# Softmax denominators of a convolution-attention block taken group by group in 64x64 tiles, two scalings and one run of silus moved

## The chip, the cores and the metric

The kernel runs on one core of one Trainium2 chip. The metric is the device time of one execution in microseconds (us), as the median of repeated runs; lower is better. Three runs of the kernel before took 2205.79, 2205.89 and 2208.82 us.

The core has a matrix engine (PE, with its weight loads shown apart as PEld), a vector engine (DVE), a scalar engine (ACT), a third engine for simple vector work (POOL) and a queue engine that mostly issues transfers (SP). Each takes its instructions strictly in order; semaphores tie the engines together. Matrix products write to PSUM, eight banks per partition; everything else lives in SBUF or in DRAM.

## The reference

All data is float32: eight images of 512 channels, 32x32 pixels. After a group norm comes one block with a residual:

```python
t = cbs(x, cv1_w, cv1_bn, 0)              # 1x1 convolution, batch norm, silu
ys = [t[:, :C], t[:, C:]]                 # C = 256
for i in range(N):                        # N = 2
    yi = ys[-1]
    z = cbs(yi, m_cv1_w[i], m_cv1_bn[i], 1)          # 3x3 convolution
    z = bot_attention(z, m_qkv_w[i], m_rw[i], m_rh[i])
    z = jax.nn.silu(bn_eval(conv2d(z, m_cv2_w[i], 0), m_cv2_bn[i]))
    ys.append(yi + z)
out = x + cbs(jnp.concatenate(ys, axis=1), cv2_w, cv2_bn, 0)

# in bot_attention: 4 heads of 64 channels, hw = 1024 positions
logits = jnp.einsum('bhdi,bhdj->bhij', q, k + r) * HD ** (-0.5)
a = jax.nn.softmax(logits, axis=-1)
out = jnp.einsum('bhij,bhdj->bhdi', a, v)
```

What matters here is the softmax: its denominator is the sum of exp(logits) over the 1024 keys j, for each of 4 heads and 1024 queries i.

## The kernel before

Images go in four pairs (loop variable `p`, images `ia` and `ib`), and each pair goes through the two rounds n = 0 and n = 1. So there are 16 attentions, one for each image and round, in the order n=0 `ia`, n=0 `ib`, n=1 `ia`, n=1 `ib` of each pair; counted from 0 in time they are called attention 0 to 15 below. Between them stand the 3x3 convolutions (L675), the q, k, v projections (`project_strassen`, a seven-product scheme, or `project_direct`), the 1x1 convolution behind each attention (`m2`, L1336), the first convolution of the next images (`strassen_cv1`, whose handle is called `nxt`) and the last convolution.

One attention (`attention_fast`, from L1058) has four **groups**: two channel blocks `c` (each with two heads) times two halves of the queries (512 each). A group has eight key blocks j of 128, taken as four **pairs**. For each key block, four matrix products in 64x64 tiles write the logits of both heads (`l_ps`, 128 keys x 1024, L1082), ACT takes the exponential into `pt` (L1086), DVE adds `pt` onto `acc` (L1100, L1103), and four products in 64x64 tiles accumulate with v (`av_ps`, L1119). Every float32 product stands as two matmul instructions in the trace, so that a key block has 8 for the logits and 8 for v, and a pair 16 and 16. The loop is skewed: the logits of pair i are issued before the product with v of pair i-1. At the end of a group ACT copies half of `av_ps` into `z`, and DVE adds the other half (L1126, L1127).

`acc` then holds sums over the eight key blocks, one for each of the 128 partitions and both heads; the sum over the partitions is still missing. `sums` (L1129) makes it with a matrix product by ones: four products per group that use all 128 rows and 32 columns each, over 256 elements, so 8 matmul instructions per group. `batch` says which groups go together: mostly (0, 1) and (2, 3); where `apart` or `at_once` is set (2,) and (3,) go alone. A group that is not the last of its batch and not in an `apart` or `at_once` attention has its last addition held back (`held_back`, L1101) until the group's `av_ps` has been evicted (L1225). ACT copies the row sums (`s_row`, L1143), SP stores them in DRAM (L1144), loads them in another layout (`total`, L1171), DVE takes the reciprocal (L1179), SP stores and loads it spread over partitions (`rs`, L1181, L1186), and DVE multiplies `z` (`scale`, L1195). `last_sums` (L1147) is another way, used in attention 0 alone (`at_once`): 64x64 tiles, two halves of the keys apart.

Where the sums stand: those of (0, 1), and of (2,) where it is alone, between the logits and the product with v of the next group (L1218, L1219); those of the last batch are called by the code after the attention (`end.sums()`), behind the first product of what follows. The groups (0, 1) are scaled inside the last group (L1214). `end.spread()` and `end.scale()` do the last batch, before `m2`.

`apart` is set for n=0 `ib` (attentions 1, 5, 9, 13); eleven attentions are plain; attention 0 is `at_once`.

The tile framework orders the instructions of each engine with a planner that simulates the engines with estimated costs, and inserts the semaphore waits and buffer releases. `tc.issue_after(ins)` only says that an instruction stands behind another on the same engine. Pools have fixed buffers by tag: three two-bank PSUM buffers `big` (logits, sums, most other products), one two-bank `av`; in SBUF `acc` 2, `h` 2 (row sums, and temporaries of the convolution's tiles), `rs` 4, `pt` 6.

Two further places belong to the change. `finish` (L1897) runs six silus on ACT for the next image's first convolution; in the n=1 attentions it is called from `middle` behind the silus of `m2` and ahead of the exponential's table load. `first_tiles` (L2188) makes the first tiles for the 3x3 convolution near the start; POOL clears two edge columns (L591, L592) that DVE needs (L619).

Of the kernel before, what the change touches and what calls it, by code (L numbers as in the profile page):

```python
# [45 lines left out]
F32 = mybir.dt.float32  # L46
# [16 lines left out]
def kernel(  # L63
# [449 lines left out]
    def stages(act, small, ps_big, ps_av, n_pt):  # L513
# [425 lines left out]
        def project_strassen(n, z, w, t, early=None, middle=None, table=False, silus=()):  # L939
# [80 lines left out]
            if table:  # L1020
                with tc.issue_after(copied.ins):
                    table_of(AF.Exp)
            ps_c, ps_w = big(), big()
# [34 lines left out]
        def attention_fast(qkv, ao, at, behind, at_once=False, apart=False):  # L1058
# [70 lines left out]
            def sums(gs):  # L1129

                NQ4 = HALF // 2
                ps = ps_big.tile([P, len(gs), NQ4], F32, tag="big", name="s_ps")
                for n, g in enumerate(gs):
                    acc = accs.pop(g)
                    for at_q in range(4):
                        hd, part = divmod(at_q, 2)
                        nc.tensor.matmul(  # L1137
                            ps[at_q * 32 : (at_q + 1) * 32, n, :], ones[:, 0:32], acc[:, hd, ts(part, NQ4)],
                            start=True, stop=True, tile_position=(0, at_q * 32),
                        )  # L1140
                s_dram = tc.dram_tile([len(gs), 4, NQ4], F32, name=f"s_dram{at + gs[0]}")
                row = act.tile([P, len(gs), NQ4], F32, tag="h", name="s_row", bufs=2)
                nc.scalar.copy(row, ps)  # L1143
                nc.sync.dma_start(s_dram.rearrange("g a i -> a g i"), row[0:P:32])  # L1144
                return s_dram

            def last_sums(g):  # L1147

                ps = ps_big.tile([P, 2, HALF], F32, tag="big", name="s_ps")
                acc = accs.pop(g)  # L1150
                for kh in range(2):
                    r = slice(kh * HD, (kh + 1) * HD)
                    for hd in range(2):
                        nc.tensor.matmul(
                            ps[hd * HD : (hd + 1) * HD, kh, :], ones[r], acc[r, hd, :],
                            start=True, stop=True,
                        )
# [8 lines left out]
            def last_total(g, s_dram):  # L1166
                cs = small.tile([P, 2, QP], F32, tag="cs", name="cs", bufs=2)
                nc.sync.dma_start(cs, s_dram.rearrange("k h (i r) -> (h i) k r", r=QP))
                nc.vector.tensor_tensor(sums_all[:, at + g, :], cs[:, 0], cs[:, 1], ALU.add)
# [6 lines left out]
            def spread(gs, s_dram):  # L1176

                rc = small.tile([P, len(gs), QP], F32, tag="rc", name="rc", bufs=2)
                inverted[0] = nc.vector.reciprocal(rc, total(gs, s_dram))  # L1179
# [23 lines left out]
            s_drams, rss, evicted = {}, {}, [None]  # L1203
            for i in range(len(pairs) + 1):
                if i < len(pairs):
                    added = logits(pairs[i])
                    g, at_q = divmod(i, NQ)
                    with tc.issue_after(added.ins):
                        if at_q == NQ - 2 and g - 1 in batch:
                            gs = batch[g - 1]  # L1210
                            rss[gs] = spread(gs, s_drams[gs])
# [20 lines left out]
            with tc.issue_after(added.ins):  # L1232
                behind.get(len(groups), lambda: None)()

            g = len(groups) - 1
            if not at_once:
                gs = batch[g]
                if apart:
                    with tc.issue_after(evicted[0].ins):
                        scale_all(batch[g - 1])  # L1240
                return SimpleNamespace(
                    evicted=evicted[0], added=added,
                    sums=lambda: s_drams.update({gs: sums(gs)}),
                    spread=lambda: rss.update({gs: spread(gs, s_drams[gs])}),
                    scale=lambda: scale_all(gs),
                )
            ps, rows, s_dram = last_sums(g)
            with tc.issue_after(added.ins):
                behind.get(len(groups) + 1, lambda: None)()
# [5 lines left out]
            return SimpleNamespace(scaled=scale(g, rs), check=lambda: last_total(g, s_dram))  # L1255
# [559 lines left out]
        def strassen_cv1(w, xts, y0s, y1, t_tile):  # L1815
# [81 lines left out]
            def finish():  # L1897
                with tc.issue_after(silu_in[-1].ins), tc.issue_after(m2_silu[0].ins):
# [289 lines left out]
    def first_tiles(g, i):  # L2188
        return s.tiles_steps(Y1[g], putter(vs, g), [i], ecs[g], ec_at=(("rs", 4), ("t", 4))[g])
# [83 lines left out]
    for p in range(NP):  # L2273
# [166 lines left out]
        if more and not direct:  # L2440
            end.sums()
            nxt.go_on()
            nxt.sums()
# [11 lines left out]
            nxt.finish()  # L2455
# [5 lines left out]
        else:  # L2461
# [30 lines left out]
            else:  # L2492
                qkv = s.project_strassen(
                    0, z[:, :, 1], take_blocks("sq", 0, 1, SQ_NAMES), t, early=end.sums, middle=middle
# [49 lines left out]
        end.sums()  # L2544
# [83 lines left out]

        def middle():
# [3 lines left out]
            if more:  # L2633
                nxt.finish()
                nxt.keep()
# [3 lines left out]
            1, z[:, :, 1], take_blocks("sq", 1, 1, SQ_NAMES), t, early=end.sums, middle=middle  # L2639
# [45 lines left out]
        if not more:  # L2685
# [30 lines left out]
            end.sums()  # L2716
# [79 lines left out]
        end.sums()  # L2796
# [148 lines left out]
```

## Time and profile before

| | before |
|---|---|
| median of three runs | 2205.89 us |
| the profiled execution's own time | 2206.25 us |
| its span in the trace | 2204.8 us |
| PE busy | 2176.4 us (99%) |
| DVE, ACT, POOL busy | 1817.5, 1094.1, 220.9 us |
| TensorE clock granted, mean | 0.999 of full speed |

The span runs from the first to the last instruction that the profiler recorded; the execution takes 1.45 us more. Matmuls are pipelined: one of 512 elements lasts about 590 ns from start to end, but the next starts long before that, so PE's cost is read from the distances between the starts of blocks, and not from the sum of durations. A row of the timeline view gives start and length in us, engine, line, operation, output<-inputs, tile shape (rows*columns) and the operand's shape, a count, and in brackets the idle time ahead of it with its releaser.

### The profile page before, as it was taken

To read this page: it belongs to the slowest core of one execution; us is meant where nothing else is said; L and a number is where in the kernel's file an instruction comes from. 1 tells how busy PE (TensorE), PEld (TensorE's weight loads), DVE (VectorE), ACT (ScalarE), POOL (GpSimd) and SP (SyncE) were. 2 spreads that over 40 slices of the span, in tenths; PEclk is the share of its full clock that TensorE was granted. 3 is DMA by queue.
4 is the path that set the end of the run, shared out by engine and by line. 5 is a ranking of instruction groups with operands and counts; after the bars stand their busy time and mean duration, and the time that the engine had idled before them with its cause. 6 is when DMAs were issued, how large, how long until landed. Compare 5 with 4: busy or idle time off the path is not lost.

```text
span 2204.8 us, 40989 instructions
## 1 busy us (share of the span) xinstructions
PE 2176.4 (99%) x16546; PEld 1117.9 (51%) x16546; DVE 1817.5 (82%) x2996; ACT 1094.1 (50%) x1320; POOL 220.9 (10%) x393
## 2 busy tenths in 40 slices
PE   7999999999999999999999999999999999999998
PEld 3653438343484444734458443564346834383436
DVE  8988879878978688986897868997788877897677
ACT  7454553554225666366314676455622465336543
POOL 4322210000210000000012000000002100000001
PEclk9999999999999999999999999999999999999999
DMA  9954447212583323612159141542126811261224
GB/s 276 323 159 143 163 149 262 84 52 74 153 287 95 118 84 127 208 51 77 57 135 330 33 165 38 184 140 78 59 68 170 301 30 45 92 204 32 76 59 116
DMA packets 135529, 291.93 MB, mean 132 GB/s; under 512 B 33732, under 2 KB 61376, under 8 KB 134308
## 3 DMA queue, kind: packets, MB, share of 16 engines
q1 hardware_dynamic: 102708, 201.01, 27.4%
q0 software_dynamic: 32624, 88.23, 13.6%
q8 instruction: 132, 2.16, 0.4%
q14 instruction: 65, 0.53, 0.1%
HBM read 219.58 MB, written 69.60 MB: 131 GB/s over the span
## 4 chain that ended last, share of the span: by engine, by line
PE 87%; DVE 8%; DMA 2%; issue 1%; ACT 1%; POOL 0%; SPq 0%; DVEq 0%; ACTq 0%; POOLq 0%
PE av_ps L1119 19%; PE l_ps L1082 18%; PE c_ps L675 10%; PE p_ps L958 7%; PE c L1356 5%; PE m_ps L1336 5%; PE c_q L1404 5%; PE x_ps L1828 4%; PE ps L545 3%; PE c L1388 3%; PE p_ps L964 3%; PE c_new L1356 2%; PE s_ps L1137 1%; DMA taps<-in_m_cv_w_dram 1%; DVE acc L1103 1%
## 5 line engine op out<-in xcount | busy, mean ns | idle before, releaser
L1086 ACT ACTIVATE pt<-l_ps 128x1024 f32<-128x1024 f32 x512 | 495.6, 1023 | 328.2 <-PE l_ps L1082 252.4
L1082 PE MATMUL l_ps<-q,kr 64*64 64x512 f32 x4096 | 485.5, 590 | 0.9 <-ACT pt L1086 0.9
L1119 PE MATMUL av_ps<-pt,vT 64*64 64x512 f32 x4096 | 484.7, 590 | 1.2 <-DVE z L1127 1.1
L1103 DVE TENSOR_TENSOR acc<-acc,pt 128x1024 f32<-128x1024 f32 x362 | 442.5, 1222 | 37.2 <-ACT pt L1086 9.8
L1119 PEld LDWEIGHTS av_ps<-pt,vT 64*64 64x64 f32 x4096 | 156.0, 133 | 280.7 <-issue 234.8
L1082 PEld LDWEIGHTS l_ps<-q,kr 64*64 64x64 f32 x4096 | 157.4, 133 | 270.3 <-issue 246.4
L675 PE MATMUL c_ps<-v_in,u 128*64 128x128 f32 x4320 | 238.5, 273 | 0.0
L675 PEld LDWEIGHTS c_ps<-v_in,u 128*64 128x64 f32 x4320 | 235.8, 137 | 4.9 <-issue 4.6
L1127 DVE TENSOR_TENSOR z<-av_ps,z 128x512 f32<-128x512 f32 x64 | 43.9, 687 | 98.6 <-ACT z L1126 98.5
L1336 PE MATMUL m_ps<-z,m_sb 128*128 128x512 f32 x256 | 114.2, 593 | 0.4 <-DVE z L1195 0.4
L958 PE MATMUL p_ps<-t_z,sq 128*128 128x512 f32 x224 | 105.9, 595 | 0.0
L680 ACT COPY c_m<-c_ps 128x512 f32<-128x512 f32 x48 | 28.1, 586 | 151.0 <-PE c_ps L675 132.7
L517 ACT ACTIVATE t<-m_ps,bh,sh 128x512 f32<-128x512 f32 x64 | 46.3, 774 | 95.4 <-PE m_ps L1336 94.2
L1100 DVE TENSOR_TENSOR acc<-pt 128x1024 f32<-128x1024 f32 x64 | 78.0, 1219 | 14.2 <-PE s_ps L1137 8.7
L958 PE MATMUL p_ps<-z,sq 128*128 128x512 f32 x168 | 81.3, 604 | 0.8 <-ACT z L517 0.7
L1336 PEld LDWEIGHTS m_ps<-z,m_sb 128*128 128x128 f32 x256 | 47.7, 190 | 57.4 <-issue 52.3
L1504 POOL DMA_DIRECT2D c_out<-in_x_dram x48 | 43.4, 1041 | 273.6 <-ACT c_out L517 271.9
L1195 DVE TENSOR_TENSOR z<-z,rs 128x512 f32<-128x512 f32 x64 | 42.2, 685 | 30.0 <-DMA rs<-r_dram 29.9
L517 ACT ACTIVATE z<-z,bh,sh 128x512 f32<-128x512 f32 x64 | 48.7, 809 | 25.2 <-DVE z L737 25.1
L958 PEld LDWEIGHTS p_ps<-t_z,sq 128*128 128x128 f32 x224 | 39.5, 191 | 36.6 <-issue 34.4
L517 ACT ACTIVATE c_out<-c,bh,sh 128x512 f32<-128x512 f32 x12 | 14.0, 1280 | 85.7 <-PE c L1388 77.7
L1828 PE MATMUL x_ps<-t_x,sw 128*128 128x512 f32 x128 | 55.9, 592 | 0.0
(409 smaller groups left out, 3326.7 us busy)
## 6 DMA issues: line engine op xcount, KB each, us to landing
u<-u SPq DMA_DIRECT2D x135, 512.0 KB
y_in<-y SPq DMA_DIRECT2D x32, 512.0 KB
rs<-r_dram SPq DMA_DIRECT2D x126, 128.0 KB
sq<-sq SPq DMA_DIRECT2D x42, 384.0 KB
x<-in_x_dram SPq DMA_DIRECT2D x28, 512.0 KB
r_in<-r SPq DMA_DIRECT2D x28, 512.0 KB
c_out<-in_x_dram POOLq DMA_DIRECT2D x56, 256.0 KB, 6.4
out_dram<-c_out POOLq DMA_DIRECT2D x56, 256.0 KB, 5.4
```

The lines of the kernel that those rows point to most:

```text
L517: silued[0] = nc.scalar.activation(dst, src, AF.Silu, scale=sh[:, k : k + 1], bias=bh[:, k : k + 1])
L675: conv_product[0] = nc.tensor.matmul(to[o], us[cp][:, k, row, c, o], rhs, start=(k == 0), stop=(k == NM - 1),)
L958: nc.tensor.matmul(ps[:, o, :], w[:, o, :], rhs, start=not onto, stop=True, skip_group_check=onto)
L1082: nc.tensor.matmul(ps[kh * HD : (kh + 1) * HD, hd, :], kr[r, c, o : o + HD], q[r, c, ts(half, HALF)], start=True, stop=True,)
L1086: last_exp[0] = exp = nc.scalar.activation(pt, ps, AF.Exp, scale=SCALE)
L1100: return nc.vector.tensor_tensor(accs[g], pt[0], pt[1], ALU.add)
L1103: ins = nc.vector.tensor_tensor(accs[g], accs[g], pt[i], ALU.add)
L1119: nc.tensor.matmul(avs[g][hd * HD : (hd + 1) * HD, kh, :], vT[r, j, o : o + HD], pt[i][r, hd, :], start=(j == 0), stop=(j == NJ - 1),)
L1336: nc.tensor.matmul(pss[half][:, oc, :], m2_sb[:, n, k, ts(oc, P)], ao[:, k, ts(half, HALF)], start=(k == 0), stop=(k == NM - 1),)
L1356: nc.tensor.matmul(ps[:, o, :], w[:, k, ts(o, P)], rhs[part][:, c], start=(k == 0 and not onto), stop=(k == KB - 1), skip_group_check=onto,)
L1404: nc.tensor.matmul(to, a[:, c], b[:, c], start=first and c == 0, stop=last and c == 1, skip_group_check=True)
L1828: nc.tensor.matmul(ps[:, o, :], w[:, c, ts(o, P)], rhs[c], start=(c == 0 and not onto), stop=(c == 1), skip_group_check=onto,)
```

## The change

1. `sums` and `total` for batches and `last_sums`, `last_total` become one `sums(g)` for one group, in the form that `last_sums` had: four products by ones with 64 rows, 64 columns and 512 elements, two for each half of the keys; two copies into `s_row`; one DMA per copy. `total` loads both halves for each group and DVE adds them.
2. Places: `sums(g)` stands ahead of a product with v of the next group, in its first pair if g ends a batch, and otherwise in its second pair. The sums of group 3 stand directly behind the last product with v, ahead of the hooks that start the following work. `end.sums()` is gone.
3. Except in attention 0, (0, 1) is scaled behind the attention and not within the last group. In `apart` attentions the spreading of group 2 moves behind the attention too, and both groups 2 and 3 are scaled by `end.scale()`.
4. In n=1 attentions of the first three image pairs the silus of `finish` stand behind the copy of v's second quarter (`copied`) and ahead of those of `m2`.
5. The first clearing in `first_tiles` goes to DVE.
6. In one path, `nxt.sums` is put behind the last addition to `acc`.

```diff
-            def sums(gs):
...
-                    for at_q in range(4):
-                        hd, part = divmod(at_q, 2)
-                        nc.tensor.matmul(
-                            ps[at_q * 32 : (at_q + 1) * 32, n, :], ones[:, 0:32], acc[:, hd, ts(part, NQ4)],
-                            start=True, stop=True, tile_position=(0, at_q * 32),
-                        )
...
-            def last_sums(g):
+            def sums(g):
                 ps = ps_big.tile([P, 2, HALF], F32, tag="big", name="s_ps")
                 acc = accs.pop(g)
                 for kh in range(2):
                     r = slice(kh * HD, (kh + 1) * HD)
                     for hd in range(2):
-                        nc.tensor.matmul(
+                        summed[0] = nc.tensor.matmul(
                             ps[hd * HD : (hd + 1) * HD, kh, :], ones[r], acc[r, hd, :],
                             start=True, stop=True,
                         )
...
                 for kh, row in enumerate(rows):
                     nc.scalar.copy(row, ps[:, kh, :])
-                    for hd in range(2):
-                        nc.sync.dma_start(s_dram[kh, hd : hd + 1, :], row[hd * HD : hd * HD + 1, :])
-                return ps, rows, s_dram
+                    nc.sync.dma_start(s_dram[kh], row[0:P:HD])
+                s_drams[g] = s_dram
+                return ps, rows
 
-            def total(gs, s_dram):
+            def total(gs):
+                cs = small.tile([P, 2, 2, QP], F32, tag="cs", name="cs", bufs=1)
+                for n, g in enumerate(gs):
+                    nc.sync.dma_start(cs[:, n], s_drams.pop(g).rearrange("k h (i r) -> (h i) k r", r=QP))
                 dst = sums_all[:, at + gs[0] : at + gs[0] + len(gs), :]
-                nc.sync.dma_start(dst, s_dram.rearrange("g a (i r) -> (a i) g r", r=QP))
+                nc.vector.tensor_tensor(dst, cs[:, : len(gs), 0], cs[:, : len(gs), 1], ALU.add)
                 return dst
...
-                        if at_q == NQ - 2 and g - 1 in batch:
+                        if at_q == NQ - 2 and g - 1 in batch and not (apart and g == 3):
...
-                        if at_q == 1 and g - 2 in batch:
+                        if at_once and at_q == 1 and g - 2 in batch:
                             scale_all(batch[g - 2])
                 if i > 0:
                     g, j0 = pairs[i - 1][0]
-                    if j0 == 0 and g - 1 in batch:
-                        s_drams[batch[g - 1]] = sums(batch[g - 1])
+                    if g > 0 and j0 == (0 if g - 1 in batch else PAIR):
+                        sums(g - 1)
                     times_v(pairs[i - 1])
...
-            with tc.issue_after(added.ins):
-                behind.get(len(groups), lambda: None)()
             g = len(groups) - 1
+            ps, rows = sums(g)
+            for at_hook in range(2):
+                with tc.issue_after(added.ins), tc.issue_after(summed[0].ins):
+                    behind.get(len(groups) + at_hook, lambda: None)()
             if not at_once:
                 gs = batch[g]
-                if apart:
-                    with tc.issue_after(evicted[0].ins):
-                        scale_all(batch[g - 1])
+                last = [batch[2], gs] if apart else [gs]
+                with tc.issue_after(added.ins):
+                    if apart:
+                        rss[last[0]] = spread(last[0])
+                with tc.issue_after(evicted[0].ins):
+                    scale_all(batch[1])
...
-            def finish():
-                with tc.issue_after(silu_in[-1].ins), tc.issue_after(m2_silu[0].ins):
+            def finish(after):
+                with tc.issue_after(silu_in[-1].ins), tc.issue_after(after.ins):
...
+            clear=nc.gpsimd if g or i else nc.vector,
...
-            end.sums()
             nxt.go_on()
-            nxt.sums()
+            nxt.sums(end.added)
...
+        def finish_cv1(copied):
+            if more:
+                nxt.finish(copied)
+                nxt.keep()
```

`project_strassen` takes `finish_cv1` as `early_silus` and calls it behind the copy of v's second quarter; the calls of `end.sums` are taken out everywhere.

More of the change, by code (lines that the diff above doesn't have):

```diff
@@ L1231, in attention_fast @@
                         behind.get(g if j0 == 0 else (g, j0 // PAIR), lambda: None)()
[L1232 to L1233 removed]
             g = len(groups) - 1
+            ps, rows = sums(g)
+            for at_hook in range(2):
+                with tc.issue_after(added.ins), tc.issue_after(summed[0].ins):
+                    behind.get(len(groups) + at_hook, lambda: None)()
             if not at_once:
                 gs = batch[g]
[L1238 to L1240 removed]
+                last = [batch[2], gs] if apart else [gs]
[4 more added lines that the diff above has]
+                    scale_all(batch[1])
                 return SimpleNamespace(
                     evicted=evicted[0], added=added,
[L1243 to L1249 removed]
+                    spread=lambda: rss.update({gs: spread(gs)}),
+                    scale=lambda: [scale_all(part) for part in last][-1],
+                )
             with tc.issue_after(evicted[0].ins):
@@ L1254, in attention_fast @@
             nc.vector.reciprocal(rs, rs)
-            return SimpleNamespace(scaled=scale(g, rs), check=lambda: last_total(g, s_dram))
+            return SimpleNamespace(scaled=scale(g, rs), check=lambda: total((g,)))
         def attention_general(n, z):
@@ L2454 @@
                 nxt.adds2()
-            nxt.finish()
+            nxt.finish(s.m2_silu[0])
             nxt.keep()
@@ L2493 @@
                 qkv = s.project_strassen(
-                    0, z[:, :, 1], take_blocks("sq", 0, 1, SQ_NAMES), t, early=end.sums, middle=middle
+                    0, z[:, :, 1], take_blocks("sq", 0, 1, SQ_NAMES), t, middle=middle
                 )
@@ L2632, in middle @@
             s.m2(1, z[:, :, 0], Y2[0], lambda oc, half: img(y3a[half][:, oc, :]))
-            if more:
-                nxt.finish()
-                nxt.keep()
             s.exp_table()
         qkv = s.project_strassen(
-            1, z[:, :, 1], take_blocks("sq", 1, 1, SQ_NAMES), t, early=end.sums, middle=middle
+            1, z[:, :, 1], take_blocks("sq", 1, 1, SQ_NAMES), t, middle=middle, early_silus=finish_cv1,
         )
```

32 lines of the change are left out of this document (10 added, 22 removed).

## The prediction

> **What bounds the kernel now.** I read the page first, and then the busy time by stretches; two of them:
>
> ```profile
> span 2204.8 us, 40989 instructions
> ...
> 0.00:100.00 100.00, 83.71 (x404) 42.78 (x406) 89.35 (x219) 67.79 (x113) 39.40 (x81) 1.00 0.91 303
> 100.00:2180.00 2080.00, 2075.68 (x16078) 1062.96 (x16075) 1715.22 (x2755) 1018.77 (x1200) 180.28 (x310) 1.00 0.39 124
> ```
>
> The columns are the stretch, its length, busy time of PE, PEld, DVE, ACT and POOL, the granted clock, DMA share and GB/s. Between 100 and 2180 us PE is idle for 4.3 of 2080 us, at full clock. All 16 attentions and all touched sums lie there. So each us of PE work that is added or taken away counts in full, work moved on DVE or ACT counts only through PE's waits, and no relief of those engines can give more than about 4 us there. What PE waits for, in total us, times and longest:
>
> ```profile
> PE gm_ps L760 <- DVE mv L754: 7.9, 1, 7.9
> PE c_ps L675 <- DVE v_in L629: 3.4, 3, 2.0
> ...
> PE av_ps L1119 <- DVE z L1127: 1.1, 2, 0.5
> PE l_ps L1082 <- ACT pt L1086: 0.9, 2, 0.5
> ...
> PE m_ps L1336 <- DVE z L1195: 0.4, 1, 0.4
> ```
>
> The first lies at the very start, ahead of all that changes; the others return below.
>
> **The cost of the sums before.** The timeline of attention 2, around the sums of groups 0 and 1 (PE's rows):
>
> ```profile
> 413.90 1.90 PE L1082 MATMUL l_ps<-q,kr 64*64 64x512 f32 x16
> ...
> 417.33 1.90 PE L1082 MATMUL l_ps<-q,kr 64*64 64x512 f32 x16
> 419.16 1.07 PE L1137 MATMUL s_ps<-acc,ones 128*32 128x256 f32 x16
> ...
> 421.93 1.90 PE L1082 MATMUL l_ps<-q,kr 64*64 64x512 f32 x16
> ```
>
> From logits to logits a pair takes 417.33 - 413.90 = 3.43 us, and 421.93 - 417.33 = 4.60 us with the sums in it: two groups' sums cost **1.17 us**. A single group's, in attention 5:
>
> ```profile
> 832.07 1.90 PE L1082 MATMUL l_ps<-q,kr 64*64 64x512 f32 x16
> 833.90 0.64 PE L1137 MATMUL s_ps<-acc,ones 128*32 128x256 f32 x8
> ...
> 836.24 1.90 PE L1082 MATMUL l_ps<-q,kr 64*64 64x512 f32 x16
> ```
>
> That is 4.17 - 3.43 = **0.74 us**. The difference of the two, 0.43 us, is a group's streaming; 0.31 us comes once per visit, for going from 64x64 tiles to 128x32 ones and back. Behind an attention the sums stand among 128x128 products (attentions 14 and 5, and the chain of waits around attention 0):
>
> ```profile
> 2040.19 1.98 PE L958 MATMUL p_ps<-z,sq 128*128 128x512 f32 x4
> 2042.10 1.07 PE L1137 MATMUL s_ps<-acc,ones 128*32 128x256 f32 x16
> 2043.11 1.98 PE L958 MATMUL p_ps<-t_z,sq 128*128 128x512 f32 x4
> 2044.93 1.05 PE L964 MATMUL p_ps<-sq,z 128*128 128x128 f32 x8
> ```
>
> ```profile
> 844.93 1.98 PE L1828 MATMUL x_ps<-x,sw 128*128 128x512 f32 x4
> 846.84 0.64 PE L1137 MATMUL s_ps<-acc,ones 128*32 128x256 f32 x8
> 847.41 8.85 PE L1828 MATMUL x_ps<-x,sw 128*128 128x512 f32 x20
> 856.10 6.17 PE L1336 MATMUL m_ps<-z,m_sb 128*128 128x512 f32 x14
> ```
>
> ```profile
> 201.50 7.06 PE ps L545 x16
> 209.59 7.06 PE ps L545 x16
> 216.65 6.87 PE m_ps L1336 x16
> ```
>
> A 128x128 instruction of 512 elements takes 6.87/16 = 0.43 us; the first block after another tile shape loses about 0.1 us more (7.06 against 6.87, the last x20 block 8.69 against 8.59), and one such loss stays, since the attention ends in 64x64 tiles in both kernels. Two groups: 4.74 - 8 x 0.43 - 0.1 = **1.20 us**. One group: 11.17 - 24 x 0.43 - 0.1 = **0.77 us**. Attention 0's own form: 15.15 - 32 x 0.43 - 0.1, about **1.2 us**. How often each occurs:
>
> ```profile
> L1137 PE MATMUL s_ps<-acc,ones x504: 379/379/404, 175.5 to 2127.3; 128*32 128x256 f32 x168
> L1143 ACT COPY s_row<-s_ps x36: 372/586/648, 176.6 to 2127.7; 128x512 f32<-128x512 f32 x27, 128x256 f32<-128x256 f32 x9
> ...
> L1154 PE MATMUL s_ps<-acc,ones x8: 589/614/640, 208.5 to 209.0; 64*64 64x512 f32 x8
> ```
>
> 27 double sums (16 within attentions, 11 behind) and 9 single ones (5 and 4), 63 groups with 8 instructions each, and one group by L1154. So: 16 x 1.17 + 5 x 0.74 + 11 x 1.20 + 4 x 0.77 + 1.2 = 18.7 + 3.7 + 13.2 + 3.1 + 1.2 = **39.9 us**.
>
> **The cost of the sums after.** A group has 8 instructions of 512 elements in 64x64 tiles, which is the form of `av_ps`. A pair takes 3.43 us for 32 such instructions, so 8 cost 0.86 us; and as they stand between products of the same tiles, I add no change of shape. L1154 agrees: its eight start within 208.5 to 209.0. 64 x 0.86 = **54.9 us**. The reason is plain in the shapes: a product over 64 rows sums half the keys, so a group streams 4 x 512 elements where 4 x 256 did. Per double visit the change saves 0.31 us and pays 2 x 0.43. The difference is **+15.0 us**, all on the bounding engine. Bounds: +12 if each of some 27 visits behind and within attentions has 0.1 us more of shape change than I found, +18 if the new blocks still show 0.05 us of seam each.
>
> The Trainium skill, TensorEngine Tiling (Array Packing), Key Properties, says that changing the tiling mode drains the engine, which speaks for this change, and the 0.31 us agree. The same page, section When to Use Tiling, gives row tiling to contractions of up to 64, and this one has 128, which speaks against it, as the 0.86 against 0.43 us do.
>
> **The sums behind the last product with v: a new wait?** PE now needs the last `acc` right at the attention's end, and everything behind it on PE (the first products of the next stage) would wait too. Attention 14, from the eviction of group 2:
>
> ```profile
> 2028.93 0.69 DVE L1127 TENSOR_TENSOR z<-av_ps,z 128x512 f32<-128x512 f32 x1 [4.30 <-ACT z L1126]
> ...
> 2034.46 1.28 DVE L1195 TENSOR_TENSOR z<-z,rs 128x512 f32<-128x512 f32 x2
> ...
> 2035.67 5.21 DVE L1103 TENSOR_TENSOR acc<-acc,pt 128x1024 f32<-128x1024 f32 x4
> 2036.08 1.94 ACT L1086 ACTIVATE pt<-l_ps 128x1024 f32<-128x1024 f32 x2 [1.54 <-PE l_ps L1082]
> 2036.65 3.61 PE L1119 MATMUL av_ps<-pt,vT 64*64 64x512 f32 x32
> ```
>
> PE is done with v at 2036.65 + 3.43 = 2040.08, DVE with `acc` at 2040.88: unchanged, PE would wait 0.8 us. But DVE runs without a break there, and its 1.28 us of scaling leave; the sums of group 2 also push PE's end out by 0.86 us. `acc` is then ready about 1.3 us ahead of PE, or 0.7 if the last exponential (ended 2038.02, later by 0.86, plus one addition of 5.21/4 = 1.3) decides. In the eleven plain attentions I take no wait. In `apart` ones there is no such push:
>
> ```profile
> 841.39 3.61 PE L1119 MATMUL av_ps<-pt,vT 64*64 64x512 f32 x32
> ...
> 843.47 2.55 DVE L1103 TENSOR_TENSOR acc<-acc,pt 128x1024 f32<-128x1024 f32 x2
> ```
>
> Here `acc` is late by 846.02 - 844.82 = 1.2 us, and scaling (1.28 us) and a small reciprocal leave: a margin of 0.1 us or a little more. In attentions 4 and 8 ACT also normalizes the next images and now copies two more row sums of 0.59 us; I give these six and attention 0 together 1.5 us (0 to 7). Within attentions the held-back addition follows the eviction (2028.93 + 0.69 + 1.3 = 2030.9), and the sums of group 2 stand four blocks of 1.72 us ahead of 2040.08, at 2033.2: no wait there.
>
> **What lies beside.** ACT makes 128 copies of 0.59 us instead of 38 (9 of them half as wide), some 55 us more in 1061 us of idle time of the long stretch; DVE gets 37 additions of a few elements; SP about twice the small DMAs, for which the chain to `rs` starts some 2 to 4 us earlier. If the row-sum buffers (tag `h`) hold up the convolution's tiles, DVE comes late for an eviction: 0 to 4 us, I take 1. In `apart` attentions the chain of group 2 now runs behind the attention together with that of group 3, 0 to 1 us each; the earlier start covers it, 0.
>
> **Gains.** The silus of `finish` stood ahead of the exponentials' table:
>
> ```profile
> 1011.39 1.28 ACT L532 ACT_TABLE_LOAD   x1
> ...
> 1013.86 1.09 PE L1082 MATMUL l_ps<-q,kr 64*64 64x512 f32 x8 [0.46 <-ACT pt L1086]
> ```
>
> The two waits of `l_ps` for `pt` (0.9 us in all, about 0.6 each from start to start) go: -1.1. The wait of `m_ps` for `z` behind attention 11 goes with the earlier chain: -0.5. The two of `av_ps` for the eviction in attentions 5 and 9 are not touched: 0 (at best -1.1). DVE waited once for POOL's clearing:
>
> ```profile
> 56.05 0.69 DVE L619 TENSOR_TENSOR w_d<-w_rows 128x512 f32<-128x512 f32 x1 [1.07 <-POOL w_rows L591]
> ```
>
> ```profile
> L591 DVE MEMSET w_rows<- x14: 85/85/85, 583.0 to 1692.6; 128x32 f32 x14
> ```
>
> DVE's own memsets take 2 x 0.085 us; the 0.9 us saved pass on to the 3.4 us in which `c_ps` waited for `v_in`: -0.9 (0 to -1).
>
> **Sum.** +15.0 + 1.5 + 1 - 1.1 - 0.5 - 0.9 = **+15 us**. Against the profiled execution (span 2204.8, its own time 2206.25 us) that gives 2221.3; the median shown is 0.4 lower, so I forecast **2220.9 us**.
>
> **Rivals.** *All waits at the end stay.* If the planner fills the freed DVE time with other work, `acc` is late as before: 11 plain by at least 0.8, 4 by 1.2, and the two of 4 and 8 among the plain by 1 more: about 16 us more, 2235. For it: DVE takes convolution pieces ahead of additions in the profile. Against it: the hooks now stand behind the last addition. *The change of shape decides (faster).* If two row halves streamed side by side at no cost over a full-row product, a group would take 0.43 us with no seam: 64 x 0.43 = 27.5 us, so -12.4 - 2.5 + 2.5, about 2193. It would decide if the eight instructions of L1154 ran in half of what `av_ps` takes; they don't, as 208.5 to 209.0 is one stride of 0.43 and a remainder. The Trainium skill's rule on the drain, taken alone, points to this side. *Absorbed (no change).* PE's idle time within attentions would have to hold 15 us; it has 4.3 in all, and I leave this for a planner that comes to a much better order.
>
> **How the numbers follow.** Forecast 0.81, waits stay 0.10, faster by shape 0.05, absorbed 0.04. The forecast's own range: 12 - 1.1 - 1.1 - 1 - 0.5 = +8 at the least, 18 + 7 + 4 - 1 = +28 at the most; it is unlikely that all bounds fall together, so I take 2213 to 2232, which holds most of it and the nearer part of the first rival. About 0.2% (4.4 us) can be told from no change: slower 0.91, within 0.04, faster 0.05.
>
> **What would show it.** Right: the group of `s_ps` in 64x64 tiles with 512 instructions; each visit adding 0.86 us from logits to logits; PE busy up by some 15 us; no row of `l_ps` waiting for `pt` at the start of attentions 7 and 11. The end wait would show as PE `s_ps` waiting for DVE `acc`. Wrong: a pair with sums under 3.43 + 0.6 us, or a span under 2210.

## The result and the profile after

The changed kernel takes **2227.64 us** (median of six runs, 2226.62 to 2228.6) against 2207.32 us of the kernel before (median of six, 2205.79 to 2208.82): a ratio of **1.0092** with an interval of 1.0079 to 1.0105. It is slower by about 20 us. The forecast was 2220.9 with a range of 2213 to 2232: sign and range hold, and the middle is 6.7 us too low.

The profiled execution of after took 2227.86 us with a span of 2226.3, so 21.5 us more span than before. Line numbers have moved: the logits are L1084, the product with v L1121, the sums L1138, the row-sum copies L1145, the scaling L1177, `m2` L1318 and the products of `c_q` L1386 (L1404 before). From the page of after, and its busy time from 100 to 2200 us (columns as in the prediction):

```profile
span 2226.3 us, 41462 instructions
```

```profile
100.00:2200.00 2100.00, 2092.16 (x16098) 1084.31 (x16098) 1722.12 (x2790) 1064.68 (x1290) 179.54 (x310) 1.00 0.39 123
```

PE still bounds everything: it is idle for 7.8 of 2100 us where it was for 4.3 of 2080. So most of the added time is PE work, and some 3.5 us are new waits. The tile view of `s_ps` shows the new work (x512 counts the instructions; the x171 behind the shape is of every third), and the timeline of attention 2 its price:

```profile
L1138 PE MATMUL s_ps<-acc,ones x512: 589/589/641, 166.7 to 2144.1; 64*64 64x512 f32 x171
L1145 ACT COPY s_row<-s_ps x128: 577/592/619, 170.0 to 2145.3; 128x512 f32<-128x512 f32 x128
```

```profile
417.11 1.90 PE L1084 MATMUL l_ps<-q,kr 64*64 64x512 f32 x16
...
420.55 1.90 PE L1084 MATMUL l_ps<-q,kr 64*64 64x512 f32 x16
422.26 1.04 PE L1138 MATMUL s_ps<-acc,ones 64*64 64x512 f32 x8
423.12 1.90 PE L1121 MATMUL av_ps<-pt,vT 64*64 64x512 f32 x16
424.84 1.90 PE L1084 MATMUL l_ps<-q,kr 64*64 64x512 f32 x16
```

A pair without sums takes 420.55 - 417.11 = 3.44 us, one with them 424.84 - 420.55 = 4.29: 0.86 us (423.12 - 422.26) for one group, with no trace of a change of shape. What PE waits for:

```profile
PE m_ps L1318 <- DVE z L1177: 3.1, 2, 2.2
...
PE c_q L1386 <- DVE m_kept L1392: 1.0, 2, 0.7
PE c_q L1386 <- DVE cz L1392: 0.8, 2, 0.5
...
PE s_ps L1138 <- DVE acc L1105: 0.2, 1, 0.2
```

The rows of `l_ps` waiting for `pt` are gone, and the feared wait of `s_ps` for `acc` is one of 0.2 us. New are 3.1 us of `m_ps` waiting for `z` (0.4 before) and 1.8 us of `c_q` (0.3 before).

From the starts of the PE instructions the spans can be cut into stretches: up to the first logits, each attention (first logits to the last product with v), and what lies between. After minus before, in us:

```
up to the first logits                          144.45 -> 146.07   +1.6
attentions: eight plain +1.41 each, attention 3 +1.34,
            7 and 11 +0.72, four apart +0.20 to +0.70,
            attention 0 +0.68                                     +17.1
behind plain attentions 2, 4, 6, 8, 14          -0.34 each
behind attentions 5 and 9 (apart)               +1.42 and +2.64
behind 1 and 13 (apart)                         +0.20 and +0.45
behind 0, 3, 7, 10, 11, 12, 15       -0.36 +0.13 +0.30 -0.44 -0.40 -0.12 +0.76
between attentions and behind the last, together                   +2.9
```

The attentions carry the loss; what lies between was to give back some 3.7 us and lost 2.9.

### The profile page after: what moved, and what is told of

It reads as the page before. It is cut to its first block, busy times and chain, and to the rows that moved or that the text cites. A ratio compares the mean times of both kernels' runs of the same rounds, so it can differ in the third digit from the quotient of the medians.

```text
span 2226.3 us, 41462 instructions
## 1 busy us (share of the span) xinstructions
PE 2195.1 (99%) x16546; PEld 1140.6 (51%) x16546; DVE 1824.7 (82%) x3034; ACT 1140.0 (51%) x1410; POOL 220.9 (10%) x391
## 4 chain that ended last, share of the span: by engine, by line
PE 80%; DVE 12%; issue 3%; DMA 2%; ACT 1%; POOL 0%; SPq 0%; DVEq 0%; ACTq 0%; POOLq 0%
PE l_ps L1084 17%; PE av_ps L1121 17%; PE c_ps L675 10%; PE p_ps L958 7%; PE c L1338 4%; PE m_ps L1318 4%; PE c_q L1386 4%; PE ps L545 4%; PE x_ps L1810 3%; PE p_ps L964 3%; DVE acc L1105 2%; PE s_ps L1138 2%; PE c L1370 2%; PE c_new L1338 1%; PE p_ps L920 1%
## 5 line engine op out<-in xcount | busy, mean ns | idle before, releaser
L1121 PE MATMUL av_ps<-pt,vT 64*64 64x512 f32 x4096 | 484.8, 589 | 1.3 <-DVE z L1129 1.1
L1084 PE MATMUL l_ps<-q,kr 64*64 64x512 f32 x4096 | 486.0, 590 | 0.0
L1121 PEld LDWEIGHTS av_ps<-pt,vT 64*64 64x64 f32 x4096 | 163.8, 133 | 277.9 <-issue 242.4
L1084 PEld LDWEIGHTS l_ps<-q,kr 64*64 64x64 f32 x4096 | 161.8, 133 | 264.5 <-issue 237.4
L1318 PE MATMUL m_ps<-z,m_sb 128*128 128x512 f32 x256 | 113.8, 593 | 3.1 <-DVE z L1177 3.1
L1318 PEld LDWEIGHTS m_ps<-z,m_sb 128*128 128x128 f32 x256 | 47.7, 190 | 61.0 <-issue 52.9
L1145 ACT COPY s_row<-s_ps 128x512 f32<-128x512 f32 x128 | 69.2, 597 | 8.1 <-PE s_ps L1138 4.3
L1486 POOL DMA_DIRECT2D c_out<-in_x_dram x48 | 43.5, 1064 | 294.6 <-ACT c_out L517 293.0
L1138 PE MATMUL s_ps<-acc,ones 64*64 64x512 f32 x512 | 67.2, 592 | 0.3 <-DVE acc L1105 0.2
L1177 DVE TENSOR_TENSOR z<-z,rs 128x512 f32<-128x512 f32 x64 | 42.2, 685 | 29.2 <-DMA rs<-r_dram 29.0
```

Of the source, the lines that this page charges most:

```text
L1084: nc.tensor.matmul(ps[kh * HD : (kh + 1) * HD, hd, :], kr[r, c, o : o + HD], q[r, c, ts(half, HALF)], start=True, stop=True,)
L1121: nc.tensor.matmul(avs[g][hd * HD : (hd + 1) * HD, kh, :], vT[r, j, o : o + HD], pt[i][r, hd, :], start=(j == 0), stop=(j == NJ - 1),)
L1138: summed[0] = nc.tensor.matmul(ps[hd * HD : (hd + 1) * HD, kh, :], ones[r], acc[r, hd, :], start=True, stop=True,)
L1318: nc.tensor.matmul(pss[half][:, oc, :], m2_sb[:, n, k, ts(oc, P)], ao[:, k, ts(half, HALF)], start=(k == 0), stop=(k == NM - 1),)
```

## The experiments

The theory (P, where an expectation uses a letter) is that of the prediction: the price of the product form on PE. The rivals: waits for `acc` that eat what the moved scaling gives, and the place of the `apart` chains. The first two runs separate form from place.

**1. The old product form in the new places.** The change as it is, but single groups take four products of 128 rows, 32 columns and 256 elements; attention 0's last group keeps its own form. With the old form come one copy and one store of the row sums for each group, and no addition of two halves.

```diff
             def sums(g):
...
+                if not (at_once and g == len(groups) - 1):
...
+                    ps = ps_big.tile([P, NQ4], F32, tag="big", name="s_ps")
+                    for at_q in range(4):
...
+                        summed[0] = nc.tensor.matmul(
+                            ps[at_q * 32 : (at_q + 1) * 32, :], ones[:, 0:32], acc[:, hd, ts(part, NQ4)],
+                            start=True, stop=True, tile_position=(0, at_q * 32),
+                        )
```

> The changed kernel with the form of the sums undone (128x32 tiles of 256 elements, one row copy and one store per group, no addition of two halves), at the new places and group by group; only the last group of attention 0 keeps the 64x64 form. Theory P (the matrix engine's price of the 64x64 form): a visit within an attention costs 0.73 us where it costs 0.86, 48 of them make -6.2 us; behind the product with v about 0.6 for 0.86, 15 of them -4; so about -10 us, 2217 to 2218 us. What is left over the kernel before, about +10, is then the batches taken apart and the new waits. Theory W (the new places and the moved scaling cost the time, by waits): no change, 2226 to 2229 us.

Measured: 2217.66 us, ratio to before 1.0042 (1.0028 to 1.0056): 10 us less than after, as the theory has it. The five runs spread from 2212.39 to 2218.59 us, so that this is good to some 3 us. Its timeline of attention 2:

```profile
416.64 1.90 PE L1084 MATMUL l_ps<-q,kr 64*64 64x512 f32 x16
418.46 0.64 PE L1139 MATMUL s_ps<-acc,ones 128*32 128x256 f32 x8
...
420.80 1.90 PE L1084 MATMUL l_ps<-q,kr 64*64 64x512 f32 x16
```

A visit for one group costs 4.16 - 3.43 = 0.73 us, 0.13 less than in the new form. The other 9.7 us above before are the rest of the change, above all that each group is taken alone: three visits of 0.73 in place of one of 1.17, +1.03 us in a plain attention. In the profile (of the fastest run, with a span only 6.1 us above before) the attentions together are 10.9 us longer than before, and what lies behind them is 3.7 shorter. After has +17.1 in the attentions: the new form adds 6.2 there, which is 48 x 0.13. In the old form a group taken alone pays its own change of shape; in the new one there is none to pay, and taking groups apart costs PE nothing there (run 2 has the same 0.86 us a group in batches). So undoing the form alone gives back only half.

**2. The new form in the old places.** The kernel before, with the 64x64 products for every group but with its old batches.

```diff
-                NQ4 = HALF // 2
-                ps = ps_big.tile([P, len(gs), NQ4], F32, tag="big", name="s_ps")
...
+                for g in gs:
+                    ps = ps_big.tile([P, 2, HALF], F32, tag="big", name="s_ps")
...
+                            nc.tensor.matmul(
+                                ps[hd * HD : (hd + 1) * HD, kh, :], ones[r], acc[r, hd, :],
```

> The kernel before with the form of the sums alone changed: 64x64 tiles, two row copies and two stores per group, in the old batches and at the old places. Theory P: two groups within an attention cost 1.72 us for 1.16 (16 times, +8.9), one 0.86 for 0.73 (5, +0.6); behind an attention, among 128x128 products, two cost about 2.1 for 1.2 (11, +9.7), one 1.22 for 0.77 (4, +1.8): about +21 us, 2228 us. Theory W: within 3 us of the kernel before.

Measured: 2241.06 us, ratio 1.0153 (1.0136 to 1.017): +33 us, 12 more than expected. The pair with two groups' sums takes 425.10 - 419.95 = 5.15 us, which is 3.43 + 2 x 0.86; the price of the products within attentions holds:

```profile
419.95 1.90 PE L1082 MATMUL l_ps<-q,kr 64*64 64x512 f32 x16
421.67 1.90 PE L1138 MATMUL s_ps<-acc,ones 64*64 64x512 f32 x16
...
425.10 1.47 PE L1082 MATMUL l_ps<-q,kr 64*64 64x512 f32 x12
```

Of the 12 us, 6.6 are waits of PE that I had not seen (these rows, less the 0.9 us of `l_ps` for `pt` that before has); the rest is not traced:

```profile
PE l_ps L1082 <- DVE q L1041: 2.8, 5, 0.6
...
PE l_ps L1082 <- ACT pt L1086: 2.5, 2, 1.2
PE x_ps L1834 <- ACT s_row L1145: 2.2, 2, 1.1
```

Two groups at once need two `big` buffers of PSUM instead of one, held until ACT has copied four row sums: `x_ps` then waits for ACT's copy. After, which goes group by group, has no such wait.

**3. Each product made twice.** If the products bound directly, doubling them adds 64 x 0.86 us.

```diff
-                        summed[0] = nc.tensor.matmul(
...
+                        for _ in range(2):
+                            summed[0] = nc.tensor.matmul(
```

> The changed kernel with each of the four products of a group's sums made twice (the same result is written again). Theory P: 64 groups x 0.86 us = +55 us, 2282 us, since the matrix engine has no idle time to take it. If part of the sums' work were hidden, clearly less, under +45 us.

Measured: 2278.93 us, ratio 1.0322 (1.0302 to 1.0343): 51.3 us above after. In attention 2 a block of 16 now takes exactly its place:

```profile
417.31 1.96 PE L1139 MATMUL s_ps<-acc,ones 64*64 64x512 f32 x16
419.02 1.96 PE L1121 MATMUL av_ps<-pt,vT 64*64 64x512 f32 x16
```

419.02 - 417.31 = 1.71 us. By the stretches, the 48 groups within attentions add 43.5 us, some 0.05 each above 0.86; the 16 behind them add 7.5 us (without the start) where 13.7 would be their price. There the longer PE work covers waits: this profile has no row of `m_ps` waiting for `z`. That points to a chain beside PE which is late by a fixed time.

**4. The scaling of groups 0 and 1 back inside plain attentions.** This takes away what the forecast relied on for a timely `acc`.

```diff
-                        if at_once and at_q == 1 and g - 2 in batch:
+                        if not apart and at_q == 1 and g - 2 in batch:
                             scale_all(batch[g - 2])
...
-                    scale_all(batch[1])
+                    if apart:
+                        scale_all(batch[1])
```

> The changed kernel with the scaling of groups 0 and 1 back within the last group in the eleven plain attentions. Theory: the waits of c_q for cz and m_kept behind attentions 7, 11 and 15 (0.5 to 1.1 us each, together about 2.3) go, since the vector engine has 1.3 us less to do there; at the attentions' end acc is about as late as the sums of group 2 push the product with v out (0.80 against 0.86 us), so the sums wait under 0.2 us each: 2225 to 2228 us. Rival (the first one of the prediction): acc is late by 0.8 us or more at eleven ends, +9 us, 2236 us.

Measured: 2231.93 us, ratio 1.0114 (1.0097 to 1.013): 4.3 us above after. Its waits of PE:

```profile
PE s_ps L1138 <- DVE acc L1105: 3.4, 4, 1.4
PE m_ps L1319 <- DVE z L1177: 2.7, 2, 2.1
...
PE c_q L1387 <- DVE m_kept L1393: 1.0, 2, 0.7
...
PE c_q L1387 <- DVE cz L1393: 0.6, 1, 0.6
```

The time lies between what I expected and the rival's 2236. The waits for `acc` come back at four attentions of the eleven (3, 7, 11 and 12): 1.4, twice 0.8, and 0.3 us. So the first rival's mechanism is real, and the moved scaling removes it but for 0.2 us. The waits of `c_q` stay though. I had put those down to the scaling behind the attention; that theory falls.

**5. The spread of group 2 back inside `apart` attentions.** This tests the place of the chain that the forecast priced at nothing.

```diff
-                        if at_q == NQ - 2 and g - 1 in batch and not (apart and g == 3):
+                        if at_q == NQ - 2 and g - 1 in batch:
...
-                    if apart:
-                        rss[last[0]] = spread(last[0])
```

> The changed kernel with the spreading of group 2 back within group 3 in the four apart attentions; its scaling stays behind the attention. Theory Q (the queue of transfers): the stores of group 3's sums no longer stand behind the loads of group 2's rs, which wait for the reciprocal; the waits of m_ps for z behind attentions 5 and 9 (1.1 and 2.3 us) and the smaller ones behind 1 and 13 go: about -4 us, 2223 to 2224 us. Rival: group 3's own chain of transfers (about 9 us) is what m_ps waits for, and the time stays at 2227 to 2228 us.

Measured: 2228.17 us, ratio 1.0096 (1.008 to 1.0111), the same as after, where 4 us less were expected. The waits of `m_ps` are gone, and the stretches behind attentions 5 and 9 shrink from 84.81 and 86.03 to 83.67 and 83.66 us. But behind attention 1 there is a new wait (timeline, rows of DVE and of PE):

```profile
296.83 2.55 DVE L1105 TENSOR_TENSOR acc<-acc,pt 128x1024 f32<-128x1024 f32 x2
301.46 0.17 DVE L1155 TENSOR_TENSOR sums_all<-cs 128x8 f32<-128x8 f32 x1 [2.08 <-DMA cs<-s_dram]
...
301.78 2.50 DVE L1105 TENSOR_TENSOR acc<-acc,pt 128x1024 f32<-128x1024 f32 x2
```

```profile
299.52 2.81 PE L1121 MATMUL av_ps<-pt,vT 64*64 64x512 f32 x24
304.43 1.12 PE L1138 MATMUL s_ps<-acc,ones 64*64 64x512 f32 x8 [2.10 <-DVE acc L1105]
305.48 5.75 PE L545 MATMUL ps<-x,w 128*128 128x512 f32 x9
```

DVE stands for 2.08 us before an addition of eight elements that needs a DMA, and the last additions to `acc` stand behind it in DVE's order; PE loses 2.10 us. The stretch grows by 3.9 us over after, nearly twice the wait. The last row shows the rest: nine products take 5.75 us where 0.43 each would be 3.9, at a granted clock of 0.57 (the seventh number behind the stretch):

```profile
305.00:309.00 4.00, 4.00 (x13) 1.59 (x6) 4.00 (x7) 1.17 (x2) 0.56 (x1) 0.57 0.71 230
```

The change's move of this chain thus avoids one wait and pays with another.

**6 and 7. The clearing alone, and the silus of `finish` alone,** each put into the kernel before.

```diff
+            clear=nc.gpsimd if g or i else nc.vector,
```

> The kernel before with the first clearing on the vector engine, nothing else. Theory: -0.5 to -0.9 us at the start, as the products with v_in at 73 us come earlier. Rival: the half clock that the changed kernel's trace shows from 82 to 86 us comes with this edit, +1.2 us. Between the two lies a third: the half clock comes and goes from run to run.

```diff
+            if early_silus:
+                early_silus(copied)
```

> The kernel before with the six silus of finish behind the copy of v's second quarter, nothing else. Theory: the waits of l_ps for pt at the start of attentions 7 and 11 go, -1.2 to -1.4 us, 2206 us. Rival: the silus delay a copy out of PSUM ahead of them and the time is the same or above.

The clearing: 2207.9 against 2207.24 us, ratio 1.0001 (0.9992 to 1.001); the interval is some 2 us wide to either side and can't tell the 0.9 us forecast from nothing. In its profile DVE's wait for POOL's clearing is gone, but `c_ps` waits 3.8 us for `v_in` where it waited 3.4, so no gain is seen there either. The silus: ratio 0.9994 (0.9985 to 1.0003), 1.6 us less by the medians, which the interval does not tell from nothing; in the trace attentions 7 and 11 are shorter by 0.69 us each and the waits of `l_ps` for `pt` are gone.

**8. Groups 2 and 3 of `apart` attentions in one chain** (one addition, one reciprocal, one store of its result), in after.

```diff
-                last = [batch[2], gs] if apart else [gs]
-                with tc.issue_after(added.ins):
-                    if apart:
-                        rss[last[0]] = spread(last[0])
+                if apart:
+                    gs = batch[2] + gs
+                last = [gs]
```

> The changed kernel with groups 2 and 3 of the four apart attentions spread together, in one chain of transfers behind the attention (one addition, one reciprocal, one store, four loads), where group 2's chain stood ahead of group 3's. Theory Q: no store of group 3 stands behind a load of group 2 that waits, so the waits of m_ps for z behind attentions 5 and 9 (1.1 and 2.3 us) go, and no load stands ahead of acc on the vector engine as in apart_spread: -3.5 to -4.5 us, 2223 to 2224 us. Rival: the transfers of group 3 take that long anyway, 2227 to 2228 us.

Measured: 2227.76 us, ratio 1.009 (1.0076 to 1.0105): a miss, no gain. Of the 3.1 us of `m_ps` waits only 0.3 remain, but others stand in their place. Behind attentions 5 and 9 (85.34 us each) these are the first two rows, `c_ps` and `x_ps`, 1.45 us for each attention; the waits for `acc` stand at attentions 3 and 7, and that of `m_ps` behind attention 15:

```profile
PE c_ps L675 <- issue: 1.6, 2, 0.8
PE x_ps L1809 <- ACT y_half L517: 1.3, 2, 0.6
...
PE s_ps L1138 <- DVE acc L1105: 0.8, 2, 0.6
...
PE m_ps L1317 <- DVE z L1177: 0.3, 1, 0.3
```

**9 and 10. The old form and batches with the rest of the change.** Double visits in 128x32 tiles, the last batch directly behind the product with v, scaling and silus as in after; once with the joint chain of run 8, once with group 2's chain ahead of group 3's.

```diff
-            def sums(g):
+            def sums(gs):
+                if at_once and gs == (len(groups) - 1,):
+                    return last_sums(gs[0])
...
+                ps = ps_big.tile([P, len(gs), NQ4], F32, tag="big", name="s_ps")
...
-                    if g > 0 and j0 == (0 if g - 1 in batch else PAIR):
-                        sums(g - 1)
+                    if j0 == 0 and g - 1 in batch:
+                        sums(batch[g - 1])
...
-            ps, rows = sums(g)
+            ps, rows = sums(batch[g])
```

> The old form (128x32 tiles) and the old batches, with everything else of the change, the last batch directly behind the product with v, and groups 2 and 3 of apart attentions spread together. From form32 (2217.7 us): eleven visits within plain attentions fall away (11 x 1.03 = -11.4 against the two single ones), five others -0.3 each, the last batch is a double again (11 x +0.43), and the waits of m_ps behind 5 and 9 (0.4 each) go: 2217.7 - 11.4 - 1.5 + 4.7 - 0.8 = 2208.7 by the medians, 2206 by the traces; so within 2204 to 2209 us, no clear difference from the kernel before. Rival: with no sums of group 2 ahead of it, the product with v ends 0.73 us earlier and waits for acc at eleven ends, 2210 to 2216 us.

> As best_joint, but with group 2 of the apart attentions spread on its own ahead of group 3, as in the changed kernel: 0.5 to 1 us above best_joint by theory Q, since one store per group comes earlier than two in 64x64 form and the waits of m_ps are short already (0.4 us each in form32).

With the joint chain: **2203.25 us, ratio 0.9977 (0.9967 to 0.9986)**, 0.2% faster than the kernel before, which I had not expected to be clear of noise; the rival's waits for `acc` at eleven ends did not come. In the profiles its span is 2.3 us below before: attentions 7 and 11, with the moved silus, are 0.69 us shorter each, and what lies behind the attentions is 1.2 shorter. With the two chains: 2206.36 us, ratio 0.9997 (0.9988 to 1.0006), 3.1 us above the joint chain where 0.5 to 1 was expected. They differ in the chain alone, its order and one store fewer, and behind attention 5 one sees it. The two chains (timeline):

```profile
852.73 0.20 DVE L1190 RECIPROCAL rc<-sums_all 128x8 f32<-128x8 f32 x1 [2.64 <-DMA sums_all<-s_dram]
...
857.89 6.68 PE L1347 MATMUL m_ps<-z,m_sb 128*128 128x512 f32 x11 [1.93 <-DVE z L1206]
```

The joint chain at the same place:

```profile
850.13 0.25 DVE L1190 RECIPROCAL rc<-sums_all 128x16 f32<-128x16 f32 x1
...
855.18 7.03 PE L1346 MATMUL m_ps<-z,m_sb 128*128 128x512 f32 x16
```

The reciprocal on which the last scaling hangs comes 2.6 us earlier, and `m_ps` runs through. The stretch takes 83.26 us with the joint chain and 87.17 with the two; the 3.9 us are the wait of 1.93 and a slow clock behind it (last section). Behind attention 9 the two differ by 0.5 us.

## Why the prediction was right, and where not

**The price on PE: right.** 0.86 us for a group without a seam was forecast, and that is what stands in the timeline, and doubled in run 3. Plain attentions were to grow by 3 x 0.86 - 1.17 = 1.41 us and did; the ends were to shrink by 1.20 - 0.86 = 0.34 us, and the five where nothing waits did so to 0.01 us. Attentions together: +17.1, with the 1.4 us of lost waits put back +18.5, less the 3.7 us that the prices give for the ends: **+14.8 against +15.0**. (Attention 1 grows by 0.20 us and not by 0.70; a wait of 0.27 us there, of `gv_ps` for `dev`, is gone in after. With these 0.5 us put back too, it is 15.3.) The prediction's sum for attention 0's own form, "about 1.2", comes to 1.29 with the terms that it prints; its end shrank by 0.36 us, which with 0.86 gives 1.22. The reason for the price, twice the streaming and a saved change of shape, is borne out by run 1. That run also shows what the one sum hides: with the groups taken apart, the old form would cost some 10 us over before as well, for three changes of shape in a plain attention where there was one.

**The sums behind the last product with v: right.** One wait of 0.2 us for `acc`, where the rival had 16 us. Run 4 shows what keeps it away: with the scaling back, four ends wait, 3.4 us together.

**The gain at attentions 7 and 11: right,** 0.7 us each against 1.1 for both.

**The step that failed: "In `apart` attentions the chain of group 2 now runs behind the attention together with that of group 3, 0 to 1 us each; the earlier start covers it, 0."** The stretches behind attentions 5 and 9 are 1.33 and 2.55 us longer than the prices of the products (0.86 - 0.77 each) explain, **3.9 us**, and both waits of `m_ps` for `z`, 0.97 and 2.16 us, stand there. Behind 13 and 1 it is 0.36 and 0.11 us; no wait of `m_ps` stands there and the joint chain of run 8 leaves them as they are, so that I can't put these to the chain. I had counted the DMAs but not their order on SP. The end of attention 5 in after, SP first:

```profile
853.53 0.34 SPq L1163 DMA_DIRECT2D r_dram<-rc  x1
855.16 1.14 SPq L1168 DMA_DIRECT2D rs<-r_dram  x2
856.40 1.08 SPq L1146 DMA_DIRECT2D s_dram<-s_row  x2
858.62 0.36 SPq L1153 DMA_DIRECT2D cs<-s_dram  x1
860.86 0.34 SPq L1163 DMA_DIRECT2D r_dram<-rc  x1
862.28 1.14 SPq L1168 DMA_DIRECT2D rs<-r_dram  x2
```

```profile
852.73 1.28 ACT L1145 COPY s_row<-s_ps 128x512 f32<-128x512 f32 x2
```

```profile
865.78 1.55 PE L1318 MATMUL m_ps<-z,m_sb 128*128 128x512 f32 x3 [0.97 <-DVE z L1177]
```

ACT had group 3's row sums ready at 852.73 + 1.28 = 854.0. SP stored them at 856.40, because group 2's two `rs` loads stand ahead of that store and waited until 855.16 for the r_dram that they read. The whole chain of group 3 runs 2.4 us late, and its end is the `z` for which `m_ps` waits. Run 5 (chain inside) and run 8 (one chain) take the wait of `m_ps` away, and runs 9 and 10 differ by 3.1 us with little else changed. No run changed the order of the DMAs alone: run 8 and the joint chain of run 9 also have one reciprocal and one store fewer for each `apart` attention. Neither 5 nor 8 made the kernel faster: each put a wait of another kind in its place.

**The rest of the ends.** `c_q` waits 1.8 us where it waited 0.3, and behind attentions 3, 7 and 15 the stretches are 2.2 us longer than the prices explain; I had allowed +1.5 for late `acc` and +1 for buffers, less 0.5 at attention 11. About the right size, but only a part is what I named: behind attention 3 (0.5 us) stands the one wait for `acc`. Behind 7 and 15 (0.6 and 1.1) stand waits of `c_q`. Run 4 speaks against the moved scaling, as they stay with it undone; what does cause them stays open, the buffers of tag `h` among the rest.

**The clearing: not shown.** I forecast -0.9 us at the start. Run 6 can't tell so little from nothing, and in its profile `c_ps` waits for `v_in` no less than before. In the profiles the first logits come after 143.4 to 146.1 us with the clearing on DVE and after 144.5 to 146.9 with it on POOL: the start varies by more than the edit could give. In after's profile 1.7 us of it are a slow clock (last section: 4 us at 0.58). The +1.6 us there are therefore no effect of the change that I can show.

Against the profiled +21.5: prices 14.8, ends 6.6 (3.9 of them from the failed step), lost waits -1.4, start +1.6. Of the miss of 6.5 us against the forecast +15, 3.9 are that step and 2.5 the start (+1.6 in place of -0.9), most of it the clock of that one execution. That the rest of the ends came out at about its size, though mostly for a cause that I had not named, was luck.

## What to carry over

On a saturated engine, price a change of tile shape by streamed elements plus the seams, each read from start to start; here the seams saved (0.31 us a visit) were worth less than the doubled streaming (0.43 us a group), and a form with seams wants its groups in batches. With the old form and the old batches in place, the rest of the change (with the joint chain) made the kernel 0.2% faster. When a step is moved on an in-order queue, write down the queue's new order instruction by instruction: a store that is ready waits behind a load that is not (2.4 us here). When a wait is removed by moving work, look at what the moved work now stands behind; two of the repairs tried here only moved the wait.

## What was not expected of the hardware

A wait of PE of about 2 us can be followed by products at half speed, which doubles its cost. Behind the wait of 1.93 us in run 10, the windows show the granted clock (the seventh number behind the stretch: 0.83, 0.50, 0.81):

```profile
857.00:859.00 2.00, 1.11 (x2) 0.64 (x3) 1.98 (x4) 0.41 (x1) 0.54 (x1) 0.83 0.90 283
859.00:861.00 2.00, 2.00 (x3) 0.67 (x2) 2.00 (x6) 0.00 (x0) 0.00 (x0) 0.50 0.99 311
861.00:863.00 2.00, 2.00 (x5) 0.91 (x4) 1.46 (x5) 0.54 (x1) 0.22 (x2) 0.81 1.01 316
```

If the clock is either 1.00 or 0.50, as these windows suggest, it was at half for 2 x 0.17 / 0.5 + 2 + 2 x 0.19 / 0.5 = 3.4 us, which loses 1.7 us. It does not follow every such wait. Behind attention 9 of after (timeline and window) the wait is longer, and twelve products take 5.42 us at full clock, where eleven take 6.68 in run 10's row above:

```profile
1411.13 5.42 PE L1318 MATMUL m_ps<-z,m_sb 128*128 128x512 f32 x12 [2.16 <-DVE z L1177]
```

```profile
1413.00:1417.00 4.00, 4.00 (x11) 1.85 (x10) 3.78 (x9) 1.86 (x3) 0.23 (x2) 1.00 1.06 349
```

And after ran slowly near the start, at a place where the kernel before did not. The windows from 82 to 86 us, first of after, then of before:

```profile
82.00:86.00 4.00, 4.00 (x48) 4.00 (x45) 4.00 (x8) 2.73 (x4) 1.15 (x2) 0.58 1.00 379
```

```profile
82.00:86.00 4.00, 4.00 (x59) 3.35 (x56) 4.00 (x9) 3.00 (x5) 0.89 (x2) 1.00 1.01 375
```

Again this is 4.00 x 0.42 / 0.5 = 3.4 us at half, and a loss of 1.7 us. The kernel before with the silus alone moved (run 7) has it there too, 0.59 from 83 to 87 us, and so it does not hang on the sums.

The Trainium skill, TensorE: Matmul & The Clock Gate, Part 1: The HAM clock gate, says that the clock halves after an idle window of about 3.4 us, counted in windows that run freely. A row of 0.50 agrees with the halving, and free windows would explain why it differs from place to place; but the two waits ahead of slow products that are shown here lasted 1.93 and 2.10 us, less than the figure of the page.
